# A selective-scan kernel: softplus from exp(v) taken out of PSUM, and the old y added where y is copied out

## The chip, the cores and the metric

The kernel runs on one core of one Trainium2 chip. The metric is device microseconds (us) of one execution: 11103.35 us before the change, the median of 3 runs (11099.11 to 11105.88). A core has TensorE (PE, matrix multiply; PEld is its loading of weights), VectorE (DVE), ScalarE (ACT, table functions), GpSimd (POOL), and SyncE (SP), whose queue issues the DMAs. Each engine works through its own instructions in order and waits for others by semaphores. SBUF is the on-chip memory of 128 partitions; PSUM is the memory that TensorE writes.

## The reference

Two layers of a vision state-space model, four images each, all in float32. The first layer takes nearly all of the time and is the one changed. For each image (64 x 64 positions, L = 4096) it normalizes, projects 192 channels to 384, and runs a selective scan in four directions k: by rows, by columns, and both backwards. The scan is

```python
delta = jax.nn.softplus(delta + delta_bias[None, :, None])
...
def step(h, inp):
    dt, ut, bt, ct = inp
    dA = jnp.exp(dt[..., None] * A_k[None])
    dBu = dt[..., None] * bt[:, :, None, :] * ut[..., None]
    h = dA * h + dBu
    y = jnp.einsum('bkdn,bkn->bkd', h, ct)
    return (h, y)
```

with 16 states n for each of 384 channels d. The y of the four directions are summed with u times D, normalized, multiplied by silu(z) and projected back. The second layer does the like with a convolution ahead and has a form of the scan of its own.

## The kernel before

`FirstLayer.run` alternates, image by image, between a stage `between` (finish the last image, project the next one) and a stage `scans`. `scans` is the subject here: it takes four stretches of some 2200 us each.

The work of one image in `scans` is 32 items. An item is one direction k and one chunk c of 512 positions; the 384 channels are ND = 3 groups of 128 partitions. Items come in pairs (k, i) and (k + 2, 7 - i), first for k = 0 and 2 (rows), then for k = 1 and 3 (columns); so item 16 of each image is the first that goes by columns. An item is 16 steps, one for each state n. The whole is written as one loop over g = 16 * item + n, and the order of instructions on PE, ACT, DVE and POOL is that in which the loop writes them (`manual_schedule`). The order on SP is left to the planner of the framework.

One step g does this:

- ACT: `b_product(g + 2)` (L716, four instructions) multiplies delta*u by B into `xT`; `decay(g + 1)` (L728, three) makes exp(delta * A) into `a`.
- PE: `turn_x(g + 1, d)` (L733) transposes `xT` into a PSUM tile `x` for each of the three channel groups; each is written after `scan(g, d)`, whose buffer it takes.
- DVE: `scan(g, d)` (L741), three instructions, h = a*h + x along the 512 positions, and a small reduction (L751) that keeps the last column as the carry for the next chunk.
- POOL: `c_product(g)` (L755) multiplies h by C in place. SP loads the rows of C for two steps at a time into `bct` (L721), each load waiting for POOL to free one of three buffers.
- PE: `add_y` (L768) transposes h of a step at least LAG = 3 steps back into the three PSUM tiles `yp`, accumulating over the 16 states: 12 transposes a step. None is done in step 3 of an item, and two steps' worth in step 4, because the `yp` of the last item are still being copied out.

Beside that, two things happen once per item.

**Old y.** y lies in DRAM and each item adds to its rows. `start_y` (L762) opens the accumulation in steps 3 and 4 by multiplying the tile `yold`, loaded from DRAM, with the identity into `yp`. `end_y` (L781) copies `yp` to `yt` on DVE in steps 2 and 3 of the next item, and SP stores it. `yold` has one buffer. It is loaded one item ahead (in the loop's order after step 5), except where the direction turns from rows to columns: there the rows to be read are spread over what the last items stored, so the load is issued in step 3, after the last `end_y`.

**Delta.** `Item.steps` lists what prepares an item's delta, by (items ahead, step, engine). v is `dp`, a matmul of 13 rows (L632) into a PSUM tile of the pool `ps_m`, two buffers shared with other small uses. softplus(v) is computed as max(v, 0) + log(1 + e) with e = exp(-|v|), the log with a correction for the rounding of 1 + e. Two items ahead: ACT takes |v| in steps 10 to 12 (L638) and the exponential in step 13 (L641), POOL makes wl = 1 + e in step 14 (L645) and dt = wl - 1 in step 15 (L649). One item ahead: ACT takes the log of wl in step 2 (L652), POOL e - dt in step 1 (L655) and adds wl in step 4 (L658); DVE `delta` (L661) computes max(v, 0) + e in steps 7 to 9, from v made a second time on PE in steps 5 to 7. The tile `e` has one buffer: the |v| of an item waits for the last `delta` of the item before it. Then delta is transposed and multiplied by u (L675, L681) in steps 10 to 13.

In the first 8 items of an image, PE and ACT also compute z for the gate (`gate_in`, `gate_out`, L794, three ACT instructions an item).

Of the kernel before, what the change touches and what calls it, by code (L numbers as in the profile page):

```python
# [10 lines left out]
F32 = mybir.dt.float32  # L11
AF = mybir.ActivationFunctionType
ALU = mybir.AluOpType
# [4 lines left out]
ND = DI // 128  # L18
CB, NC2 = 96, 2
LC = 512  # L20
# [382 lines left out]
class FirstLayer:  # L403
# [168 lines left out]
    def scans(self):  # L572
        nc, tc = self.tc.nc, self.tc
        with ExitStack() as ctx:
            pool = lambda name, bufs, **k: ctx.enter_context(tc.tile_pool(name=name, bufs=bufs, **k))
            p1, p2, p3, p7 = pool("b1", 1), pool("b2", 2), pool("b3", 3), pool("b7", 7)
            pk = pool("ca", 2)
            ps_y = pool("psy", 1, space=bass.MemoryType.PSUM)
            ps_x = pool("psx", 3, space=bass.MemoryType.PSUM)
            ps_m = pool("psm", 2, space=bass.MemoryType.PSUM)  # L580
            ident = self.ident
            n8 = LC // HW

            def along(ap, k):
# [5 lines left out]
            def rows(tile_, dram, k, c):  # L590

                if k % 2 == 0:
                    return [(tile_, dram[c * LC : (c + 1) * LC, :].rearrange("(j p) e -> p j e", p=128))]
                v = dram.rearrange("(h w) e -> w h e", w=HW)[c * n8 : (c + 1) * n8]
                v = v.rearrange("(j s) h e -> s h j e", s=2)
                return [(tile_[s * HW : (s + 1) * HW], v[s]) for s in range(2)]

            def load(name, dram, k, c):
                t = p1.tile([128, NJ, DI], F32, name=name)
                for to, of in rows(t, dram, k, c):  # L600
                    nc.sync.dma_start(to, of)
                return t

            class Item:
# [27 lines left out]
                    nc.tensor.matmul(self.dp[d], w, self.xd[0 : DR + 1, :], start=True, stop=True)  # L632


                def absolute(self, d):
                    if d == 0:
                        self.e = p1.tile([128, ND, LC], F32, name="e")
                    nc.scalar.activation(self.e[:, d, :], self.dp[d], AF.Abs)  # L638

                def exp(self):  # L640
                    nc.scalar.activation(self.e, self.e, AF.Exp, scale=-1.0)  # L641

                def plus(self):
                    self.wl = p1.tile([128, ND, LC], F32, name="wl")
                    nc.gpsimd.tensor_scalar(self.wl, self.e, 1.0, 1.0, ALU.add, ALU.mult)  # L645

                def minus(self):
                    self.dt = p2.tile([128, ND, LC], F32, name="dt")
                    nc.gpsimd.tensor_scalar(self.dt, self.wl, -1.0, 1.0, ALU.add, ALU.mult)  # L649

                def log(self):
                    nc.scalar.activation(self.wl, self.wl, AF.Ln)  # L652

                def rest(self):
                    nc.gpsimd.tensor_tensor(self.e, self.e, self.dt, ALU.subtract)  # L655

                def total(self):
                    nc.gpsimd.tensor_tensor(self.e, self.e, self.wl, ALU.add)  # L658

                def delta(self, d):  # L660
                    nc.vector.scalar_tensor_tensor(  # L661
                        self.dt[:, d, :], self.dp[d], 0.0, self.e[:, d, :], ALU.max, ALU.add
                    )

                def load_u(self):
# [19 lines left out]
                def steps(self):  # L685

                    s = lambda f, *a: (lambda: f(*a))
                    r = [(3, 12, "pool", self.load_rows), (2, 0, "pe", self.turn_b), (2, 1, "dve", self.keep_b)]
                    for d in range(ND):
                        r += [(2, 7 + d, "pe", s(self.dt_rows, d)), (2, 10 + d, "act", s(self.absolute, d))]  # L690
                    r += [(2, 13, "act", self.exp), (2, 14, "pool", self.plus), (2, 14, "pool", self.load_u)]
                    r += [(2, 15, "pool", self.minus), (1, 2, "act", self.log)]
                    r += [(1, 1, "pool", self.rest), (1, 4, "pool", self.total)]
                    for d in range(ND):
                        r += [(1, 5 + d, "pe", s(self.dt_rows, d)), (1, 7 + d, "dve", s(self.delta, d))]
                    for b in range(ND):
                        r += [(1, 10 + b, "pe", s(self.turn, b)), (1, 11 + b, "dve", s(self.times_u, b))]
                    return r
# [4 lines left out]
            items = []  # L703
# [50 lines left out]
                it, n = flat[g]  # L754
                nc.gpsimd.tensor_tensor(hs[g], hs[g], bc(cs[g - n % 2][:, n % 2, :], 1, ND), ALU.mult)  # L755

            def start_y(it, b):

                if b == 0:
                    it.yp = [ps_y.tile([128, LC], F32, name=f"yp{i}") for i in range(ND)]  # L760
                yo = it.yold.rearrange("p j e -> p (j e)")[:, b * LC : (b + 1) * LC]
                nc.tensor.matmul(it.yp[b], ident, yo, start=True, stop=False, skip_group_check=True)  # L762

            def add_y(g, b):
                it, n = flat[g]
                for i in range(NJ):
                    j, d = divmod(b * NJ + i, ND)
                    nc.tensor.matmul(  # L768
                        it.yp[b][:, i * 128 : (i + 1) * 128],
                        hs[g][:, d, j * 128 : (j + 1) * 128],  # L770
                        ident,
                        start=False,
                        stop=n == NS - 1,
                        is_transpose=True,
                        skip_group_check=True,
                    )

            def end_y(it, b):
                if b == 0:
                    it.yt = p1.tile([128, NJ, DI], F32, name="yt")  # L780
                nc.vector.tensor_copy(it.yt.rearrange("p j e -> p (j e)")[:, b * LC : (b + 1) * LC], it.yp[b])  # L781
                if b == ND - 1:
                    for of, to in rows(it.yt, self.y_dram, it.k, it.c):
                        nc.sync.dma_start(to, of)
# [13 lines left out]
            with tc.manual_schedule(engines={nc.tensor.engine, nc.scalar.engine, nc.vector.engine, nc.gpsimd.engine}):  # L798
# [15 lines left out]
                        if e == engine:  # L814
                            f()

                items[0].yold = load("yold", self.y_dram, items[0].k, items[0].c)
                c_rows(0)
                b_product(0)
                b_product(1)  # L820
# [3 lines left out]
                LAG = 3  # L824
                late = []
                for g in range(N + LAG + 1):
                    i, n = divmod(g, NS)
                    it = items[i] if g < N else None
                    before = items[i - 1] if i > 0 else None
                    prepare(g, "act")  # L830
                    if g + 2 < N:
                        if g % 2 == 0:
                            c_rows(g + 2)
                        b_product(g + 2)
                    if g + 1 < N:
                        decay(g + 1)
                    adds = [[] for _ in range(ND)]
                    if it is not None:
                        for at, b in (((LAG, 1), 0), ((LAG, 2), 1), ((LAG + 1, 0), 2)):
                            if at[0] == n:  # L840
                                adds[at[1]].append((start_y, it, b))

                    ready = [x for x in late if x <= g - LAG and (n > LAG or x // NS < i)][:2]
                    for j, (x, b) in enumerate((x, b) for x in ready for b in range(ND)):
                        adds[j // len(ready)].append((add_y, x, b))
                    late = [x for x in late if x not in ready]
                    for d in range(ND):
                        if g < N:
                            scan(g, d)
                        if d == 1:  # L850
                            prepare(g, "dve")
                        if before is not None and (n, d) in ((LAG - 1, 2), (LAG, 0), (LAG, 1)):
                            end_y(before, {2: 0, 0: 1, 1: 2}[d])
                            if (n, d) == (LAG, 1) and it is not None and it.yold is None:
                                it.yold = load("yold", self.y_dram, it.k, it.c)
                        if g + 1 < N:
                            turn_x(g + 1, d)
                        for f, *a in adds[d]:
                            f(*a)
                    if g < N:  # L860
                        prepare(g, "pe")
                        c_product(g)
                        late.append(g)
                        prepare(g, "pool")
                        if n == 5 and i + 1 < len(items) and items[i + 1].k % 2 == it.k % 2:
                            q = items[i + 1]
                            q.yold = load("yold", self.y_dram, q.k, q.c)


    def finish(self, batches):  # L870
# [762 lines left out]
```

## Time and profile before

| what | value |
|---|---|
| median of 3 runs | 11103.35 us |
| profiled execution, its own time | 11106.54 us |
| its span, first to last instruction | 11104.6 us |
| mean granted TensorE clock | 0.939 |
| busy: DVE, ACT, PE, POOL | 9693.3, 9775.8, 9551.9, 8587.9 us |
| items | 128, of 16 steps each |
| scans on DVE (L741) | 6144 of about 1.2 us |

The profile is one execution taken by the hardware profiler. A group of instructions is given as line, engine, operation, out<-in with the program's tile names, shapes and count; then busy us and mean ns of one; then the idle time of the engine just before them and what ended it. Instructions of one engine overlap a little, so that the mean of one is larger than the busy time over the count. In the list of waits a line reads "who waited <- for whom: us in total, times, longest". One fp32 matmul is two PE instructions in the records. The engines' shares are averages over stages; the stages between the images are other work.

### The profile page before, as it was taken

What the parts mean: (1) busy time and instruction counts of PE and PEld (TensorE: products, weight loads), DVE (VectorE), ACT (ScalarE), POOL (GpSimd) and SP (SyncE); (2) the same over time, 40 slices, a digit from 0 to 9 for tenths busy, and PEclk for the clock granted to TensorE, in tenths of its full rate; (3) what the DMA queues carried; (4) which work ended last, traced back from release to release, by engine and by line L of the source; (5) the groups of instructions that cost most, each with busy time, mean ns of one, the idle gap of its engine ahead of it and who ended that gap; (6) DMA issues with size and microseconds to landing.
All of it is one profiled execution on the core that took longest, in us unless ns stands there. A gap on an engine that the chain in (4) does not pass through costs nothing. (4 is left out here: it accounts for less than half of the span.)

```text
span 11104.6 us, 172135 instructions
## 1 busy us (share of the span) xinstructions
PE 9551.9 (86%) x61449; PEld 7273.6 (66%) x61449; DVE 9693.3 (87%) x11515; ACT 9775.8 (88%) x16979; POOL 8587.9 (77%) x2776
## 2 busy tenths in 40 slices
PE   7998888888988888888988888889988888788677
PEld 4776666666776666656776666657766766655366
DVE  4999899976999899968999899949998999878675
ACT  5999999977999999969999999959999999856477
POOL 3999899955999899938999899929998999700370
PEclk8999999998999999998999999989999999989688
DMA  4333344344333344443333433353333434433458
GB/s 125 109 108 101 91 101 101 98 137 127 109 106 101 92 101 99 98 159 112 109 103 96 98 97 99 93 168 109 109 99 95 98 98 98 120 119 123 157 131 272
DMA packets 833671, 1267.54 MB, mean 114 GB/s; under 512 B 102026, under 2 KB 517655, under 8 KB 832292
## 3 DMA queue, kind: packets, MB, share of 16 engines
q1 hardware_dynamic: 827940, 1250.15, 40.5%
q0 software_dynamic: 4864, 6.29, 0.4%
q8 instruction: 488, 8.00, 0.3%
q14 instruction: 379, 3.10, 0.1%
HBM read 955.83 MB, written 300.42 MB: 113 GB/s over the span
## 5 line engine op out<-in xcount | busy, mean ns | idle before, releaser
L755 POOL TENSOR_TENSOR h<-h,bct 128x1536 f32<-128x1536 f32 x2048 | 7062.9, 3470 | 579.9 <-DVE carry L751 477.5
L741 DVE TENSOR_TENSOR_SCAN h<-a,carry,x 128x512 f32<-128x512 f32 x5376 | 6604.9, 1266 | 231.0 <-PE x L733 194.9
L733 PE MATMUL x<-ident,xT 128*128 128x128 f32 x24576 | 4000.8, 287 | 811.8 <-DVE h L741 710.1
L716 ACT ACTIVATE xT<-dtuT,bT 128x384 f32<-128x384 f32 x8192 | 4358.8, 609 | 93.0 <-PE x L733 87.3
L733 PEld LDWEIGHTS x<-ident,xT 128*128 128x128 f32 x24576 | 2804.0, 145 | 2136.5 <-DVE h L741 920.5
L728 ACT ACTIVATE a<-dt,A_log_f 128x512 f32<-128x512 f32 x6144 | 3977.7, 716 | 0.0
L768 PE MATMUL yp<-ident,h 128*128 128x128 f32 x24576 | 3703.1, 277 | 9.2 <-POOL h L755 9.2
L768 PEld LDWEIGHTS yp<-ident,h 128*128 128x128 f32 x24576 | 2944.2, 144 | 78.8 <-issue 62.6
L632 PE MATMUL dp<-xd,w_dtb_f 13*128 13x512 f32 x1536 | 882.7, 657 | 216.0 <-DVE dt L661 211.3
L741 DVE TENSOR_TENSOR_SCAN h<-a,x 128x512 f32<-128x512 f32 x768 | 899.1, 1207 | 191.3 <-PE x L733 114.0
L645 POOL TENSOR_SCALAR wl<-e 128x1536 f32<-128x1536 f32 x128 | 189.2, 1478 | 799.3 <-ACT e L641 406.2
L519 PE MATMUL pp<-xT,w_in 96*128 96x512 f32 x1152 | 539.2, 617 | 1.1 <-DVE xw L562 1.1
L632 PEld LDWEIGHTS dp<-xd,w_dtb_f 13*128 13x128 f32 x1536 | 235.0, 189 | 456.6 <-DVE dt L661 341.3
L762 PE MATMUL yp<-yold,ident 128*128 128x512 f32 x768 | 445.1, 664 | 72.7 <-DMA yold<-y 72.7
L1137 DVE SCALAR_TENSOR_TENSOR acc<-pad,conv_w_s,acc 128x2048 f32<-128x2048 f32 x192 | 439.3, 2342 | 53.5 <-ACT acc L1135 52.9
L638 ACT ACTIVATE e<-dp 128x512 f32<-128x512 f32 x384 | 224.7, 585 | 269.3 <-DVE dt L661 155.4
L1118 POOL MEMSET pad<- 128x66 f32 x12 | 1.9, 158 | 578.4 <-DVE acc L1137 458.9
L658 POOL TENSOR_TENSOR e<-e,wl 128x1536 f32<-128x1536 f32 x128 | 445.1, 3477 | 0.3
L655 POOL TENSOR_TENSOR e<-e,dt 128x1536 f32<-128x1536 f32 x128 | 442.9, 3460 | 0.3
L751 DVE TENSOR_REDUCE carry<-h 128x3 f32<-128x3 f32 x2048 | 322.7, 158 | 70.4
L519 PEld LDWEIGHTS pp<-xT,w_in 96*128 96x128 f32 x1152 | 221.3, 198 | 244.4 <-issue 234.3
L661 DVE SCALAR_TENSOR_TENSOR dt<-dp,e 128x512 f32<-128x512 f32 x384 | 255.5, 666 | 65.2 <-POOL e L658 58.7
(170 smaller groups left out, 6875.3 us busy)
## 6 DMA issues: line engine op xcount, KB each, us to landing
bct<-xp SPq DMA_DIRECT2D x1024, 512.0 KB, 4.9
uT<-uT SPq DMA_DIRECT2D x64, 768.0 KB, 4.7
yold<-y SPq DMA_DIRECT2D x64, 768.0 KB, 7.9
y<-yt SPq DMA_DIRECT2D x64, 768.0 KB, 4.5
uT<-uT SPq DMA_DIRECT2D x128, 384.0 KB, 5.0
yold<-y SPq DMA_DIRECT2D x128, 384.0 KB, 5.3
y<-yt SPq DMA_DIRECT2D x128, 384.0 KB, 4.6
zg<-gate SPq DMA_DIRECT2D x64, 768.0 KB, 6.3
```

Of the source, the lines that this page charges most:

```text
L519: self.tc.nc.tensor.matmul(pp, self.w_in[:, i, e * 128 : (e + 1) * 128], self.xT[:, i, t * LC : (t + 1) * LC], start=(i == 0), stop=(i == ...
L632: nc.tensor.matmul(self.dp[d], w, self.xd[0 : DR + 1, :], start=True, stop=True)
L655: nc.gpsimd.tensor_tensor(self.e, self.e, self.dt, ALU.subtract)
L658: nc.gpsimd.tensor_tensor(self.e, self.e, self.wl, ALU.add)
L716: nc.scalar.mul(xTs[g][:, j, :], it.dtuT[:, j * DI : (j + 1) * DI], it.bT[:, j, n : n + 1])
L728: nc.scalar.activation(as_[g][:, d, :], it.dt[:, d, :], AF.Exp, scale=scale)
L733: nc.tensor.transpose(xs[g, d][:, j * 128 : (j + 1) * 128], xTs[g][:, j, d * 128 : (d + 1) * 128], ident)
L741: nc.vector.tensor_tensor_scan(along(hs[g][:, d, :], it.k), along(as_[g][:, d, :], it.k), along(xs.pop((g, d)), it.k), 0.0 if it.first els ...
L755: nc.gpsimd.tensor_tensor(hs[g], hs[g], bc(cs[g - n % 2][:, n % 2, :], 1, ND), ALU.mult)
L762: nc.tensor.matmul(it.yp[b], ident, yo, start=True, stop=False, skip_group_check=True)
L768: nc.tensor.matmul(it.yp[b][:, i * 128 : (i + 1) * 128], hs[g][:, d, j * 128 : (j + 1) * 128], ident, start=False, stop=n == NS - 1, is_tr ...
L1137: nc.vector.scalar_tensor_tensor(acc, part(tap), weight(tap), acc, ALU.mult, ALU.add)
```

## The change

In softplus, e becomes exp(v) instead of exp(-|v|), taken by ACT straight out of PSUM in steps 10 to 12, where |v| was taken. The exponential over 1536 columns in step 13 is gone. POOL takes m = min(e, 1) in step 13 and dt = (m + 1) - 1 in step 15; ACT takes log(e + 1), with the one as a bias, in step 2; POOL's two tensor operations give the correction m - dt and its sum with the log. `delta` becomes max(min(that, 30), v). The steps of the other operations stay.

The matmuls of `start_y` are gone: the first `add_y` of an item starts the accumulation, and `end_y` on DVE adds `yold` where it copied before. `yold` is loaded in step 8 of the item that it belongs to, for every item alike, and is read in steps 2 and 3 of the next one.

```diff
-                def absolute(self, d):
+                def exp(self, d):
                     if d == 0:
                         self.e = p1.tile([128, ND, LC], F32, name="e")
-                    nc.scalar.activation(self.e[:, d, :], self.dp[d], AF.Abs)
-
-                def exp(self):
-                    nc.scalar.activation(self.e, self.e, AF.Exp, scale=-1.0)
-
-                def plus(self):
-                    self.wl = p1.tile([128, ND, LC], F32, name="wl")
-                    nc.gpsimd.tensor_scalar(self.wl, self.e, 1.0, 1.0, ALU.add, ALU.mult)
-
-                def minus(self):
+                    nc.scalar.activation(self.e[:, d, :], self.dp[d], AF.Exp)
+
+                def cap(self):
+                    self.m = p1.tile([128, ND, LC], F32, name="m")
+                    nc.gpsimd.tensor_scalar(self.m, self.e, 1.0, 1.0, ALU.min, ALU.mult)
+
+                def rounded(self):
                     self.dt = p2.tile([128, ND, LC], F32, name="dt")
-                    nc.gpsimd.tensor_scalar(self.dt, self.wl, -1.0, 1.0, ALU.add, ALU.mult)
+                    nc.gpsimd.tensor_scalar(self.dt, self.m, 1.0, -1.0, ALU.add, ALU.add)
 
                 def log(self):
-                    nc.scalar.activation(self.wl, self.wl, AF.Ln)
+                    nc.scalar.activation(self.e, self.e, AF.Ln, bias=one)
 
                 def rest(self):
-                    nc.gpsimd.tensor_tensor(self.e, self.e, self.dt, ALU.subtract)
+                    nc.gpsimd.tensor_tensor(self.m, self.m, self.dt, ALU.subtract)
 
                 def total(self):
-                    nc.gpsimd.tensor_tensor(self.e, self.e, self.wl, ALU.add)
+                    nc.gpsimd.tensor_tensor(self.e, self.e, self.m, ALU.add)
 
                 def delta(self, d):
                     nc.vector.scalar_tensor_tensor(
-                        self.dt[:, d, :], self.dp[d], 0.0, self.e[:, d, :], ALU.max, ALU.add
+                        self.dt[:, d, :], self.e[:, d, :], 30.0, self.dp[d], ALU.min, ALU.max
                     )
...
-                        r += [(2, 7 + d, "pe", s(self.dt_rows, d)), (2, 10 + d, "act", s(self.absolute, d))]
-                    r += [(2, 13, "act", self.exp), (2, 14, "pool", self.plus), (2, 14, "pool", self.load_u)]
-                    r += [(2, 15, "pool", self.minus), (1, 2, "act", self.log)]
+                        r += [(2, 7 + d, "pe", s(self.dt_rows, d)), (2, 10 + d, "act", s(self.exp, d))]
+                    r += [(2, 13, "pool", self.cap), (2, 14, "pool", self.load_u)]
+                    r += [(2, 15, "pool", self.rounded), (1, 2, "act", self.log)]
...
-            def start_y(it, b):
-
-                if b == 0:
-                    it.yp = [ps_y.tile([128, LC], F32, name=f"yp{i}") for i in range(ND)]
-                yo = it.yold.rearrange("p j e -> p (j e)")[:, b * LC : (b + 1) * LC]
-                nc.tensor.matmul(it.yp[b], ident, yo, start=True, stop=False, skip_group_check=True)
-
             def add_y(g, b):
                 it, n = flat[g]
+                if n == 0 and b == 0:
+                    it.yp = [ps_y.tile([128, LC], F32, name=f"yp{i}") for i in range(ND)]
                 for i in range(NJ):
...
-                        start=False,
+                        start=n == 0 and i == 0,
...
-                nc.vector.tensor_copy(it.yt.rearrange("p j e -> p (j e)")[:, b * LC : (b + 1) * LC], it.yp[b])
+                part = slice(b * LC, (b + 1) * LC)
+                yt, yo = (t.rearrange("p j e -> p (j e)")[:, part] for t in (it.yt, it.yold))
+                nc.vector.tensor_add(yt, it.yp[b], yo)
...
-                items[0].yold = load("yold", self.y_dram, items[0].k, items[0].c)
...
-                        for at, b in (((LAG, 1), 0), ((LAG, 2), 1), ((LAG + 1, 0), 2)):
-                            if at[0] == n:
-                                adds[at[1]].append((start_y, it, b))
...
-                            if (n, d) == (LAG, 1) and it is not None and it.yold is None:
-                                it.yold = load("yold", self.y_dram, it.k, it.c)
...
-                        if n == 5 and i + 1 < len(items) and items[i + 1].k % 2 == it.k % 2:
-                            q = items[i + 1]
-                            q.yold = load("yold", self.y_dram, q.k, q.c)
+                        if n == 8:
+                            it.yold = load("yold", self.y_dram, it.k, it.c)
```

More of the change, by code (lines that the diff above doesn't have):

```diff
@@ L580, in scans @@
             ps_m = pool("psm", 2, space=bass.MemoryType.PSUM)
-            ident = self.ident
+            ident, one = self.ident, self.one
             n8 = LC // HW
@@ L837, in scans @@
                     adds = [[] for _ in range(ND)]
-                    if it is not None:
-                        for at, b in (((LAG, 1), 0), ((LAG, 2), 1), ((LAG + 1, 0), 2)):
-                            if at[0] == n:
-                                adds[at[1]].append((start_y, it, b))
                     ready = [x for x in late if x <= g - LAG and (n > LAG or x // NS < i)][:2]
```

## The prediction

> **What bounds the kernel.** I read the page's shares first:
>
> ```profile
> PE 9551.9 (86%) x61449; PEld 7273.6 (66%) x61449; DVE 9693.3 (87%) x11515; ACT 9775.8 (88%) x16979; POOL 8587.9 (77%) x2776
> ```
>
> Four engines lie close together, so shares alone choose no bound. The windows view, with one window from the first scan of an item to that of the next, goes further: item 2 (which has a gate), item 12, item 21, and item 16, the first by columns.
>
> ```profile
> 319.80:390.90 71.10, 64.22 (x433) 50.87 (x432) 66.17 (x75) 69.00 (x122) 64.62 (x21) 0.95 0.40 106
> 1011.60:1080.30 68.70, 60.06 (x419) 47.29 (x419) 65.61 (x75) 66.31 (x118) 64.73 (x21) 0.98 0.37 99
> 1643.20:1710.30 67.10, 58.43 (x419) 45.64 (x420) 65.46 (x76) 65.16 (x116) 64.74 (x21) 1.00 0.41 101
> 1283.70:1369.90 86.20, 62.77 (x419) 48.98 (x420) 63.10 (x75) 65.53 (x117) 64.54 (x20) 0.84 0.33 87
> ```
>
> Columns: window, length, busy us of PE, PEld, DVE, ACT, POOL, granted clock, DMA. Item 21, at full clock, lasts 67.10 us with DVE busy 65.46: little is left. Item 12 has 3.1 us of DVE idle. Item 2 has ACT at 69.00 of 71.10. Item 16 loses some 18 us outright. The waits view says for what:
>
> ```profile
> DVE h L741 <- PE x L733: 308.9, 446, 18.0
> ACT e L638 <- DVE dt L661: 155.4, 108, 2.6
> PE yp L762 <- DMA yold<-y: 72.7, 4, 18.4
> ```
>
> DVE waits for transposes, not for ACT; ACT itself waits once an item, at the first |v| of step 10, for the single buffer `e`. So an ordinary item is DVE's, and ACT is a close second. The timeline of item 16 shows the third line:
>
> ```profile
> 1307.42 17.54 SPq L601 DMA_DIRECT2D yold<-y  x4
> ...
> 1317.03 2.07 PE L762 MATMUL yp<-yold,ident 128*128 128x512 f32 x2 [18.07 <-DMA yold<-y]
> ...
> 1320.06 1.22 DVE L741 TENSOR_TENSOR_SCAN h<-a,x 128x512 f32<-128x512 f32 x1 [17.70 <-PE x L733]
> ```
>
> The load is issued after the last `end_y`, behind a `bct` load in SP's queue; `start_y` waits for it at the head of PE's queue, the transposes behind it, and DVE for those.
>
> The prices, from the groups of instructions:
>
> ```profile
> L762 PE MATMUL yp<-yold,ident 128*128 128x512 f32 x768 | 445.1, 664 | 72.7 <-DMA yold<-y 72.7
> L681 DVE TENSOR_TENSOR dtuT<-tp,uT 128x512 f32<-128x512 f32 x384 | 259.0, 674 | 18.8 <-PE tp L675 8.7
> L781 DVE COPY yt<-yp 128x512 f32<-128x512 f32 x384 | 258.2, 674 | 17.7 <-PE yp L768 17.4 <-issue 0.3
> L645 POOL TENSOR_SCALAR wl<-e 128x1536 f32<-128x1536 f32 x128 | 189.2, 1478 | 799.3 <-ACT e L641 406.2 <-DMA xp<-xw 393.1
> L641 ACT ACTIVATE e<-e 128x1536 f32<-128x1536 f32 x128 | 189.2, 1478 | 0.3
> ```
>
> Last, two windows of 3.4 us in step 3 of item 11:
>
> ```profile
> 954.40:957.80 3.40, 1.26 (x11) 0.85 (x9) 3.40 (x4) 3.40 (x7) 3.40 (x2) 1.00 0.22 71
> 957.80:961.20 3.40, 3.40 (x10) 1.98 (x9) 3.37 (x5) 3.40 (x7) 3.40 (x2) 0.50 0.98 281
> ```
>
> PE was busy for 1.26 us (37%); the next window ran at half clock.
>
> **What the Trainium skill says.** "TensorE: Matmul & The Clock Gate", section "What's actually happening": the clock is halved after a quiet window of a free-running 3413 ns grid and restored after a busy one. The trace agrees: changes come in steps of 3.413 us. From its clock and matmul records I worked out the thresholds here, leaving L632's 13-row matmuls aside: all 62 full-clock windows of the scans with PE busy below 35% were followed by half clock, 68 of 82 at 35 to 40%, 6 of 44 at 40 to 45%, nearly none above 50%. At half clock, all 75 windows busy below 80% were followed by another at half. "VectorE: DVE Perf Modes", "Why PSUM operands drop a tier": with a PSUM operand, fp32 runs at one element a cycle; hence a copy from PSUM should cost what an addition costs, and L781 and L681 are both 674 ns. "ScalarE: Activation LUTs", "What ACT_TABLE_LOAD costs": functions cost alike, a pointer operand about 93 ns more; L638 without one is 585 ns, L794 with a bias pointer 681.
>
> **The change, part by part**, against the profiled 11106.5 us (span 11104.6 and 1.9 around it; 3.2 above the median).
>
> 1. *The stall at the turn to columns goes.* The load no longer gates PE: it has from step 8 to step 2 of the next item, over 40 us, and its median landing takes 5 to 8 us. Item 16 averages 85.2 us over the four images. Without the wait I put it at 66.7, between item 30 (65.9, almost nothing prepared) and the usual 68.2. Gain 4 x 18.5 = 74. Bounds: 17.7 and 20 an item, 70 to 80.
>
> 2. *ACT loses L641 and gains a pointer*: -1.48 + 0.09 = -1.39 us an item. In items 8 to 29, which are DVE's (DVE idle 2.6 us an item, of it about 1.65 for PE in steps 9 to 11), this lengthens ACT's wait at `e` and gives almost nothing; 0.1 for the small gaps in steps 1 and 5, x 84 = 8. Items 1 to 7 are ACT's: they average 69.3 us with 3.9 us of DVE idle, the excess of 1.3 lying in steps 0, 1, 3 and 5. I take 1.1 x 28 = 31 (bounds 0.6 and 1.3: 17 to 36). Exp from PSUM costs what |v| did.
>
> 3. *Start of each image*: `e` lies on the path to the first scan twice (item 0's delta; item 1's exponential ahead of `b_product(0)` on ACT), 1.48 each: 4 x 2.96 = 12.
>
> 4. *DVE*: three additions for three copies, and `delta` with its operands exchanged (the second layer's L1376 also reads SBUF first and PSUM second: 678 ns against L661's 666). Nothing; 0.01 us x 6 x 128 = 8 at most. There is no cover for this on DVE.
>
> 5. *POOL*: two one-input operations for two, 1.48 each; the first a step earlier. POOL runs without a pause from step 14 to about step 9, and `total` (L658) ends a median 0.4 us ahead of `delta`. Starting at step 13 rather than 14 uses one step's slack, 3.77 - 3.47 = 0.30, so the margin becomes 0.7 us. The log no longer waits for POOL's second operation (20.4 us in all, hidden). Minimum on POOL is nowhere in this trace: below, 1.48; above, the two-input 3.47. I take 1.48.
>
> 6. *PE loses* six L762 records an item, 445.1/128 = 3.5 us, in steps 3 and 4. PE is behind only in steps 4 to 6 there (DVE's wait in step 5: 0.05 us, counted above); the waits of steps 9 to 11 start from L632, which waits for the `delta` that frees `ps_m`. They stay. But step 3 becomes emptier. In item 12 PE is free from 1024.06 to the transposes of step 4 at 1029.9, but for three groups of transposes of 0.63 us, 1.8 apart; a window there holds two, 1.26 us. By the thresholds nearly nine items in ten will go to half clock in or just after step 3, where 34 of 127 did. Half clock from about 1028.3 or later ends after one window, and PE, 3 us less loaded than before, still meets its scans. If it starts earlier (1.3 of the 3.41 us of phase, 38%), its first window stays under 80% busy, and half clock lasts 6.8 us, through step 4. There 4 transposes take 0.86: from 1029.87 come 4 transposes and 8 adds to 1032.5, 4 to 1033.3, 8 to about 1034.7, and the third group of x is there at 1035.3, against the scan's 1034.85. Some 0.5 us late: 0.38 x 0.5 x 128 = 25 lost. Bounds: 0, and 0.9 in every item, 115.
>
> 7. *SP*: as many loads as before; in the built programs `yold` stands at the same place in SP's queue for row items (after the store of `yt` and one `bct`). Nothing queued behind it moves.
>
> Sum: -74 - 8 - 31 - 12 + 25 = -100: 11006 for a profiled execution, 11003 as a median; I say 11000, 0.9% faster.
>
> **Rivals.** (a) *ACT is the bound throughout.* Then every item gains 1.39: 124 x 1.39 = 172, with 74 and 12: 10850. For it: ACT has the largest share. Against: item 21, DVE 65.46 of 67.10, and ACT waiting in step 10. (b) *Half clock spreads*: the 0.9 us of part 6 in every item takes back 115: -125 + 115, about 11090. For it: some six in ten items more come into that state, and DVE has no slack. Against: PE's work in step 4 falls by 2 us. (c) *PE's relief shortens the waits of steps 9 to 11* too, or half clock costs nothing: 0.4 x 124 more, 10950. (d) *Slower: the minimum on POOL.* At 3.47 us, `total` passes its 0.7 us margin by 1.3 and `delta`, DVE's own instruction, waits as much in every item: 124 x 1.3 = 161, so 11106 - 100 + 161 - 3 = 11164. It costs from 2.2 us on and cancels the gain at 3.0. "GPSIMD Engine Reference", "Elementwise — side-by-side cycle accounting", has bodies of up to two operations at about one cycle per element, which fits L645's 1478 ns, but data-dependent branches at 12; I hold a minimum for the former. (e) That `yold` is still waited for: it would show as before, 70 us worse; the 40 us speak against it.
>
> **Chances.** My forecast 0.66, with its own range 10965 to 11045; (a) 0.05; (b) 0.11; (c) 0.10; (d) 0.07; (e) 0.01. The range to hold 8 in 10: 10935 to 11080. About 0.2%, 22 us, is what a measurement of this kernel can tell from no change. Faster: the forecast, (a), (c), and half of (b), 0.87; within: the rest of (b), 0.06; slower: 0.07.
>
> **What will show it.** Right: no wait of PE for `yold`, item 16 under 68 us, items 1 to 7 at about 68, L781's mean near 674 and POOL's new L645 near 1478, a lower mean clock than 0.939 with half clock in step 3 of most items, and ACT's wait at `e` grown to about 3 us. Wrong: `delta` waiting for POOL (d), DVE waiting for x in step 5 by nearly 1 us (b), or ordinary items at 67 or less (a, c).

## The result, and the profile after

The changed kernel takes 11943.1 us, the median of 4 runs (11940.04 to 11948.4), against 11101.23 us for the kernel before in the same comparison. The ratio is 1.0762, 95% interval 1.0749 to 1.0775: 7.6% slower, where 0.9% faster was forecast.

The first line of the page after, the shares of the engines over the span of 11938.1 us:

```profile
PE 9833.7 (82%) x60681; PEld 7595.2 (64%) x60681; DVE 9746.0 (82%) x11515; ACT 9643.7 (81%) x16851; POOL 9572.8 (80%) x2776
```

DVE and ACT are busy for about as long as before. POOL has as many instructions, 2776, and 985 us more. The groups say which (line, engine, operation, out<-in, shapes, count, then busy us and mean ns, then idle time before and its releaser):

```profile
L647 POOL TENSOR_SCALAR dt<-m 128x1536 f32<-128x1536 f32 x128 | 690.8, 5397 | 0.7
L643 POOL TENSOR_SCALAR m<-e 128x1536 f32<-128x1536 f32 x128 | 689.5, 5387 | 780.1 <-ACT e L639 398.3 <-DMA xp<-xw 381.8
...
L776 DVE TENSOR_TENSOR yt<-yp,yold 128x512 f32<-128x512 f32 x384 | 258.8, 675 | 21.4 <-PE yp L761 17.9 <-issue 0.7
L659 DVE SCALAR_TENSOR_TENSOR dt<-e,dp 128x512 f32<-128x512 f32 x384 | 257.3, 671 | 406.8 <-POOL e L656 400.2 <-PE dp L632 6.5
```

The two one-input operations on POOL, `cap` (L643) and `rounded` (L647), take 5.39 and 5.40 us each, where L645 and L649 took 1.48. The addition of the old y (L776) costs what the copy cost, 675 ns, and `delta` 671. The windows view of one ordinary item, 20, from its first scan to that of the next (window, length, busy us of PE, PEld, DVE, ACT, POOL, clock, DMA):

```profile
1698.40:1774.50 76.10, 62.54 (x413) 49.84 (x414) 66.16 (x76) 65.01 (x117) 72.44 (x21) 0.91 0.34 89
```

Items 18 to 29 last 76.00 us on average against 68.18 before. DVE's work in one has hardly changed, 66.16 us (65.46 and 65.61 in the two items shown before); POOL is now the longest, at 72.44, but not without a pause: it too stands for 3.7 us of the item. The waits view shows how POOL's work reaches DVE, first in the changed kernel (who waited <- for whom: us in total, times, longest):

```profile
DVE h L739 <- PE x L731: 739.8, 744, 4.9
...
DVE dt L659 <- POOL e L656: 400.2, 123, 23.3
...
PE yp L761 <- POOL h L753: 311.7, 128, 4.3
```

and in the kernel before:

```profile
DVE dt L661 <- POOL e L658: 58.7, 4, 16.9
...
PE yp L768 <- POOL h L755: 9.2, 8, 2.2
```

Both waits come once an item now. The two timelines of item 20, POOL's and then the one of the engines that follow it, give the order:

```profile
1682.38 3.47 POOL L753 TENSOR_TENSOR h<-h,bct 128x1536 f32<-128x1536 f32 x1 [1.09 <-DVE carry L749]
1686.81 3.47 POOL L753 TENSOR_TENSOR h<-h,bct 128x1536 f32<-128x1536 f32 x1 [0.95 <-DVE carry L749]
1691.11 3.47 POOL L753 TENSOR_TENSOR h<-h,bct 128x1536 f32<-128x1536 f32 x1 [0.83 <-DVE carry L749]
1694.56 5.38 POOL L643 TENSOR_SCALAR m<-e 128x1536 f32<-128x1536 f32 x1
1699.92 6.89 POOL L753 TENSOR_TENSOR h<-h,bct 128x1536 f32<-128x1536 f32 x2
1706.78 5.39 POOL L647 TENSOR_SCALAR dt<-m 128x1536 f32<-128x1536 f32 x1
```

```profile
1722.37 10.26 POOL L753 TENSOR_TENSOR h<-h,bct 128x1536 f32<-128x1536 f32 x3
...
1725.87 0.66 PE L761 MATMUL yp<-ident,h 128*128 128x128 f32 x4 [2.91 <-POOL h L753]
...
1727.07 1.28 DVE L739 TENSOR_TENSOR_SCAN h<-a,carry,x 128x512 f32<-128x512 f32 x1 [2.60 <-PE x L731]
...
1732.58 3.45 POOL L656 TENSOR_TENSOR e<-e,m 128x1536 f32<-128x1536 f32 x1
...
1736.07 0.69 DVE L659 SCALAR_TENSOR_TENSOR dt<-e,dp 128x512 f32<-128x512 f32 x1 [1.94 <-POOL e L656]
```

Just before step 13 POOL has caught up and waits for DVE; from step 13 on it falls behind. By step 6 its products are late, so `add_y` waits at the head of PE's queue, the transposes of x behind it, and a scan behind those; in step 7 `delta` waits for `total`. So what counts is not how busy POOL is over the item, but how late it is where others wait for it. The stall at the turn to columns is gone all the same: item 16 lasts 73.7 us, less than its neighbours.

### The profile page after: what moved, and what is told of

Its sections match the earlier page's. It is cut to its first block, busy times and chain, and to the rows that moved or that the text cites. A ratio compares the mean times of both kernels' runs of the same rounds, so it can differ in the third digit from the quotient of the medians.

```text
span 11938.1 us, 170647 instructions
## 1 busy us (share of the span) xinstructions
PE 9833.7 (82%) x60681; PEld 7595.2 (64%) x60681; DVE 9746.0 (82%) x11515; ACT 9643.7 (81%) x16851; POOL 9572.8 (80%) x2776
## 5 line engine op out<-in xcount | busy, mean ns | idle before, releaser
L731 PE MATMUL x<-ident,xT 128*128 128x128 f32 x24576 | 4230.5, 299 | 1206.7 <-DVE h L739 1111.3
L731 PEld LDWEIGHTS x<-ident,xT 128*128 128x128 f32 x24576 | 2973.3, 151 | 2492.8 <-DVE h L739 1220.8
L761 PE MATMUL yp<-ident,h 128*128 128x128 f32 x24576 | 3963.0, 291 | 311.7 <-POOL h L753 311.7
L761 PEld LDWEIGHTS yp<-ident,h 128*128 128x128 f32 x24576 | 3173.2, 152 | 342.3 <-POOL h L753 342.0
L643 POOL TENSOR_SCALAR m<-e 128x1536 f32<-128x1536 f32 x128 | 689.5, 5387 | 780.1 <-ACT e L639 398.3
L632 PE MATMUL dp<-xd,w_dtb_f 13*128 13x512 f32 x1536 | 1022.9, 755 | 153.4 <-DVE dt L659 148.8
L647 POOL TENSOR_SCALAR dt<-m 128x1536 f32<-128x1536 f32 x128 | 690.8, 5397 | 0.7
L659 DVE SCALAR_TENSOR_TENSOR dt<-e,dp 128x512 f32<-128x512 f32 x384 | 257.3, 671 | 406.8 <-POOL e L656 400.2
L653 POOL TENSOR_TENSOR m<-m,dt 128x1536 f32<-128x1536 f32 x128 | 444.2, 3470 | 0.3
L656 POOL TENSOR_TENSOR e<-e,m 128x1536 f32<-128x1536 f32 x128 | 442.7, 3459 | 0.3
```

What stands on the lines that cost most here:

```text
L643: nc.gpsimd.tensor_scalar(self.m, self.e, 1.0, 1.0, ALU.min, ALU.mult)
L647: nc.gpsimd.tensor_scalar(self.dt, self.m, 1.0, -1.0, ALU.add, ALU.add)
L653: nc.gpsimd.tensor_tensor(self.m, self.m, self.dt, ALU.subtract)
L656: nc.gpsimd.tensor_tensor(self.e, self.e, self.m, ALU.add)
L731: nc.tensor.transpose(xs[g, d][:, j * 128 : (j + 1) * 128], xTs[g][:, j, d * 128 : (d + 1) * 128], ident)
L761: nc.tensor.matmul(it.yp[b][:, i * 128 : (i + 1) * 128], hs[g][:, d, j * 128 : (j + 1) * 128], ident, start=n == 0 and i == 0, stop=n == N ...
```

## The experiments

**1. The price of a pair of operations.** A row of POOL instructions on a scratch tile was put at the end of the kernel before:

```diff
+    with tc.tile_pool(name="probe", bufs=1) as pp:
+        src = pp.tile([128, 1536], F32, name="src")
+        nc.gpsimd.memset(src, 0.5)
+        nc.gpsimd.tensor_scalar(pp.tile([128, 1536], F32, name="q_add_mult"), src, 1.0, 1.0, ALU.add, ALU.mult)
...
+        nc.gpsimd.tensor_scalar(pp.tile([128, 1536], F32, name="q_min"), src, 1.0, None, ALU.min)
...
+        nc.gpsimd.tensor_scalar(pp.tile([128, 512], F32, name="q512_min_mult"), src[:, :512], 1.0, 1.0, ALU.min, ALU.mult)
```

> The kernel before with a row of POOL instructions on a scratch tile put at its end, one for each pair of operations, to price the forms by themselves. If the pair of operations sets the price: (add, mult) about 1.48 us on 1536 columns; (min, mult) and (add, add) about 5.4 us, as in the changed kernel; the 512-column ones a third of that and a fixed part. If POOL's price in the changed kernel comes from its surroundings (what else uses SBUF at the time) and not from the form, all pairs cost about 1.48 us here. Which single operations are cheap is open. Total: before, and some 60 us for the row.

The one execution took 11166.31 us, 61 more than the kernel before. Its groups, one instruction each; the tile's name tells the pair:

```profile
L1547 POOL TENSOR_SCALAR q_min_mult<-src 128x1536 f32<-128x1536 f32 x1 | 5.4, 5393 | 0.0
L1549 POOL TENSOR_SCALAR q_add_add<-src 128x1536 f32<-128x1536 f32 x1 | 5.4, 5392 | 0.0
...
L1555 POOL TENSOR_SCALAR q_add<-src 128x1536 f32<-128x1536 f32 x1 | 4.1, 4077 | 0.0
...
L1564 POOL TENSOR_SCALAR q_add_add<-src 128x512 f32<-128x512 f32 x1 | 1.9, 1921 | 0.0
...
L1545 POOL TENSOR_SCALAR q_add_mult<-src 128x1536 f32<-128x1536 f32 x1 | 1.5, 1464 | 0.0
L1550 POOL TENSOR_SCALAR q_mult_mult<-src 128x1536 f32<-128x1536 f32 x1 | 1.5, 1463 | 0.0
L1546 POOL TENSOR_SCALAR q_mult_add<-src 128x1536 f32<-128x1536 f32 x1 | 1.5, 1462 | 0.0
...
L1565 POOL TENSOR_SCALAR q_add_mult<-src 128x512 f32<-128x512 f32 x1 | 0.6, 607 | 0.0
```

| operations on 1536 columns | us |
|---|---|
| (add, mult), (mult, add), (mult, mult) | 1.46 |
| (add, add), (min, mult), (max, mult), (mult, min), (add, min), (subtract, mult), (mult, subtract), (add, subtract) | 5.37 to 5.39 |
| one operation alone: min, add or mult | 4.08 |
| two tensors: add or subtract | 3.41 |

The price hangs on the pair: in these 72 us PE, DVE and ACT together were busy for under 5. A column costs (1464 - 607)/1024 = 0.84 ns in a cheap pair and (5392 - 1921)/1024 = 3.39 ns in a dear one. A single operation is dearer than a pair with a multiplication by 1.

**2. The two halves apart.** One kernel takes only the half with the old y, the other only softplus; each is the diff of the change, cut in two.

```diff
-            def start_y(it, b):
...
-                nc.vector.tensor_copy(it.yt.rearrange("p j e -> p (j e)")[:, b * LC : (b + 1) * LC], it.yp[b])
+                nc.vector.tensor_add(yt, it.yp[b], yo)
```

> Only the half of the change that concerns the old y; softplus as before. Theory 1 (POOL's two one-input operations are the whole loss): the forecast of this half stands, 74 us gained at the turn to columns, up to 25 lost to half clock: about 11030 to 11050. Theory 2 (the emptier step 3 and its half clock, or the late load of the old y, are a good part of the loss): slower than before, 11200 or more.

```diff
-                    nc.gpsimd.tensor_scalar(self.wl, self.e, 1.0, 1.0, ALU.add, ALU.mult)
...
+                    nc.gpsimd.tensor_scalar(self.m, self.e, 1.0, 1.0, ALU.min, ALU.mult)
...
+                    nc.gpsimd.tensor_scalar(self.dt, self.m, 1.0, -1.0, ALU.add, ALU.add)
```

> Only the softplus half; the old y as before. Theory 1: all of the loss is here: about 840 above before and some 50 to 70 more for the stall that is back, 11990 to 12010, unless the stall hides in POOL's backlog. Theory 2: under 11700.

The y half: 11078.56 us against 11104.97, ratio 0.9972 (0.9961 to 0.9984), a gain of 26 us and not 55 to 75. The softplus half: 11954.24, ratio 1.0765 (1.0747 to 1.0783). So the loss lies in the second. The y half has the stall's gain (item 16 from 85.17 to 65.77 us), but its items 8 to 15 are 0.76 us longer than before and items 18 to 29 0.48, and half clock begins in step 3 or 4 of 126 of its 128 items: more is lost there than the 25 us forecast. The softplus half is also faster than was expected of it (11990 to 12010): it keeps the stall of item 16 (91.8 us), yet its other items are some 0.2 to 1.0 us shorter than those of the changed kernel. Less half clock goes with that (mean clock 0.915 against 0.891); that it is the reason was not tried.

**3. Only the form of the two operations.** First, the changed kernel with both in the form (add 0, mult 1):

```diff
-                    nc.gpsimd.tensor_scalar(self.m, self.e, 1.0, 1.0, ALU.min, ALU.mult)
+                    nc.gpsimd.tensor_scalar(self.m, self.e, 0.0, 1.0, ALU.add, ALU.mult)
...
-                    nc.gpsimd.tensor_scalar(self.dt, self.m, 1.0, -1.0, ALU.add, ALU.add)
+                    nc.gpsimd.tensor_scalar(self.dt, self.m, 0.0, 1.0, ALU.add, ALU.mult)
```

> The changed kernel with both one-input POOL operations in the form (add 0, mult 1), so that m = e and dt = e and the correction of the log's rounding is left out; same number, order and shapes of instructions. Theory 1: POOL's two at 1.48 us again and the forecast comes true: 10960 to 11045. Theory 3 (the new order of softplus, the exponential out of PSUM or the earlier first POOL operation is the cause, not the price of the form): stays near 11900.

11048.16 us, ratio 0.9948 (0.9931 to 0.9965): 3 us above the window that theory 1 gave, and 895 us below the changed kernel. Then one of the two dear:

```diff
-                    nc.gpsimd.tensor_scalar(self.dt, self.m, 1.0, -1.0, ALU.add, ALU.add)
+                    nc.gpsimd.tensor_scalar(self.dt, self.m, 0.0, 1.0, ALU.add, ALU.mult)
```

> The changed kernel with the first POOL operation left as it is, (min, mult), and the second as (add 0, mult 1), so that the correction comes to nothing: one of the two at 5.39 us. If POOL's chain has a margin of 0.7 us an item and each microsecond beyond it is one of the item's: 3.91 - 0.7 = 3.2 in 124 items over 11048, about 11445. If the slack that POOL has in steps 10 to 14 takes up more of it: under 11250. If each slow operation cost half of the whole: 11495.

11421.25 us, ratio 1.0287 (1.0271 to 1.0303): 373 us over the run with none, 3.0 an item where 3.2 were expected; the second dear operation adds 522 more, 4.2 an item. The first costs less than the 3.91 us by which it is dearer, as a chain with a margin has it. The second costs more than that. With one, `delta` waits for `total` in every item (347.5 us in all, 124 times), but PE waits only 10.4 us for POOL's h; its 311.7 us come with the second. What else is in the 0.3 us was not tried. Last, the reverse, the kernel before with its pairs changed and nothing else:

```diff
-                    nc.gpsimd.tensor_scalar(self.wl, self.e, 1.0, 1.0, ALU.add, ALU.mult)
+                    nc.gpsimd.tensor_scalar(self.wl, self.e, 1.0, 0.0, ALU.add, ALU.add)
...
-                    nc.gpsimd.tensor_scalar(self.dt, self.wl, -1.0, 1.0, ALU.add, ALU.mult)
+                    nc.gpsimd.tensor_scalar(self.dt, self.wl, -1.0, 0.0, ALU.add, ALU.add)
```

> The kernel before with one thing changed: its two POOL operations add 0 where they multiplied by 1, so (add, add) for (add, mult), with the same values. If the pair's price is the cause by itself: POOL has 7.82 us more an item, its margin before delta is 0.4, so 7.4 in 124 items, 920 more, about 12020, less up to 70 where the stall of item 16 hides in it. If the loss of the changed kernel needed something else of the change: well under 11900.

11946.06 us, ratio 1.0768 (1.075 to 1.0785), as slow as the changed kernel, by one constant and one opcode in each of two instructions, with the same values. That is 847 us more than before, where 920, less up to 70, were expected; the stall did not hide (item 16 lasts 92.65 us), and items 18 to 29 are 7.16 us longer, not 7.4. Its groups:

```profile
L649 POOL TENSOR_SCALAR dt<-wl 128x1536 f32<-128x1536 f32 x128 | 689.2, 5384 | 0.7
L645 POOL TENSOR_SCALAR wl<-e 128x1536 f32<-128x1536 f32 x128 | 689.1, 5383 | 795.1 <-ACT e L641 600.5 <-DMA xp<-xw 194.6
...
L652 ACT ACTIVATE wl<-wl 128x1536 f32<-128x1536 f32 x128 | 189.8, 1483 | 829.9 <-POOL dt L649 829.9
```

Here the wait sits elsewhere: ACT's log writes the tile that POOL's second operation reads, and ACT stands for 829.9 us. Where the wait shows depends on the order of softplus; that there is one comes from POOL's price, since nothing else was changed.

**4. The change with cheap pairs.** m = (e + 1) * 1, dt = (m - 1) * 1, the log of m in place, the correction e - dt; the cap at 1 is left out.

```diff
-                    nc.gpsimd.tensor_scalar(self.m, self.e, 1.0, 1.0, ALU.min, ALU.mult)
+                    nc.gpsimd.tensor_scalar(self.m, self.e, 1.0, 1.0, ALU.add, ALU.mult)
...
-                    nc.gpsimd.tensor_scalar(self.dt, self.m, 1.0, -1.0, ALU.add, ALU.add)
+                    nc.gpsimd.tensor_scalar(self.dt, self.m, -1.0, 1.0, ALU.add, ALU.mult)
...
-                    nc.scalar.activation(self.e, self.e, AF.Ln, bias=one)
+                    nc.scalar.activation(self.m, self.m, AF.Ln)
...
-                    nc.gpsimd.tensor_tensor(self.m, self.m, self.dt, ALU.subtract)
+                    nc.gpsimd.tensor_tensor(self.e, self.e, self.dt, ALU.subtract)
```

> The changed kernel with POOL's two operations written in the pairs that the probe found cheap: m = (e + 1) * 1, dt = (m - 1) * 1, the log of m in place, e - dt as the correction. The cap at 1 is left out: for v above 0 the correction is then that of 1 + e itself, at most half a unit in the last place of e. Theory 1 (the price of the form is the whole loss): as with both in (add, mult) before, 11048, within 15. If the missing correction of that run, or its log beside POOL, had helped it: nearer to 11100.

11038.68 us, ratio 0.9949 (0.9936 to 0.9963). This is the change without its cap, 65 us faster than the kernel before. To the same kernel three matmuls were added in step 3, one after each group of transposes, into a tile that is overwritten:

```diff
+            def warm(it):
+                if it.yp is None:
+                    it.yp = [ps_y.tile([128, LC], F32, name="yp0")]
+                nc.tensor.matmul(it.yp[0], ident, it.dt[:, 0, :], start=True, stop=True)
...
+                    if n == LAG and it is not None:
+                        for d in range(ND):
+                            adds[d].append((warm, it))
```

> The last kernel, and three matmuls of 512 columns in step 3 of each item, one after each group of transposes, into a PSUM tile that the next accumulation overwrites: PE does as much as in the kernel before, but nothing waits for it. If half clock after the emptied step 3 costs the 0.5 to 0.8 us that ordinary items are longer than before: 60 to 90 less than the last, 10960 to 10990, and no half clock in steps 3 and 4. If half clock there costs only what DVE is seen to wait in step 5 (0.17 to 0.3 us): 20 to 35 less, 11015 to 11030. If it costs nothing: no less, or a little more for the added matmuls.

11009.08 us, ratio 0.9919 (0.9906 to 0.9933), 30 us less for more work. In the run of part 3 with both pairs cheap, half clock began in step 3 or 4 of 124 of 128 items (37 in the kernel before), and so it did in the kernel with cheap pairs; here in none. The windows view of item 20, first without, then with the added matmuls:

```profile
1556.40:1626.00 69.60, 60.20 (x413) 48.85 (x414) 65.93 (x76) 65.36 (x118) 64.62 (x21) 0.93 0.40 97
```

```profile
1546.40:1615.20 68.80, 60.54 (x419) 47.16 (x420) 65.67 (x76) 65.07 (x117) 64.61 (x21) 0.98 0.41 98
```

DVE's work is the same within 0.3 us; the clock is 0.98 for 0.93 and the item 0.8 shorter. On average items 8 to 15 and 18 to 29 are 0.40 us shorter and items 1 to 7 0.65; DVE's idle time in step 5, 0.26 to 0.45 us an item, falls to 0.03. In total the 30 us fit the second of the run's expectations, but they are a difference: these items gain some 50 us, while items 16 and 17 become 1.3 and 1.7 us longer and the stretches between and after the images some 12 in all. So half clock seems to cost an ordinary item rather more than DVE's wait in step 5.

**5. Two versions that leave out more.** With the added matmuls kept, the second v on PE and DVE's three deltas were dropped, first together with POOL's four operations, then without those:

```diff
+                def log(self):
+                    self.dt = p2.tile([128, ND, LC], F32, name="dt")
+                    nc.scalar.activation(self.dt, self.e, AF.Ln, bias=one)
...
-                    for d in range(ND):
-                        r += [(1, 5 + d, "pe", s(self.dt_rows, d)), (1, 7 + d, "dve", s(self.delta, d))]
```

> The last kernel with delta = log(exp(v) + 1) written by ACT straight into dt: POOL's four operations, DVE's three deltas, the second v on PE and with them the correction of the log's rounding and the guard for large v are left out. If DVE bounds an ordinary item, with the waits of steps 9 to 11 that start from the delta: 3 x 0.57 of DVE and 1.65 of waits fewer in 124 items, 420 less, about 10550. If ACT takes over at its 65.3 us an item: about 330 less, 10650. If POOL's load were the bound even at 1.48 us: over 10 us an item less.

```diff
-                    nc.gpsimd.tensor_tensor(self.e, self.e, self.m, ALU.add)
+                    nc.gpsimd.tensor_tensor(self.dt, self.e, self.m, ALU.add)
...
-                    for d in range(ND):
-                        r += [(1, 5 + d, "pe", s(self.dt_rows, d)), (1, 7 + d, "dve", s(self.delta, d))]
```

> The kernel with the cheap pairs and the three added matmuls, in which POOL's last operation writes log + correction straight into dt: DVE's three deltas and the second v on PE go, the correction of the log's rounding stays, the guard for large v is left out. If the gain of the log-only kernel came from DVE and from the waits of steps 9 to 11, and not from POOL's four operations: 10580 to 10650, the rest being POOL's chain. If POOL's 10 us an item were what was gained there: near 11009 less the 210 of DVE, 10800.

10576.56 us, ratio 0.9526 (0.9512 to 0.9541), and 10601.92 us, ratio 0.9554 (0.9538 to 0.9569). The first lies between what was expected with DVE as the bound (10550) and with ACT (10650); the second lies where it should if POOL's operations were not what was gained. The windows view of item 20 of the first and of the second:

```profile
1475.30:1540.30 65.00, 56.83 (x413) 44.54 (x414) 63.59 (x72) 65.00 (x118) 55.47 (x16) 1.00 0.47 104
```

```profile
1486.00:1550.90 64.90, 56.83 (x413) 44.55 (x414) 63.58 (x73) 64.90 (x118) 64.52 (x21) 1.00 0.44 104
```

ACT is busy without a pause in both, so it is the bound there, at 65 us; POOL's four operations, 9 us of an item, cost an ordinary item nothing at their cheap prices. The 25 us between the two come from the start of the images (38 us longer in the second; the rest is 13 shorter). The second keeps the correction of the log's rounding, but lacks the cap at 1 and the guard for large v. That matters: worked out in fp32, the correction is off by up to 2 for about half of the v from 16.6 to 17.3, which the maximum with v hides in the kernel with cheap pairs and nothing hides here. As timings, both beat the kernel before and the changed one.

## Why the prediction was wrong

**The step that failed is part 5, "two one-input operations for two, 1.48 each".** It took shape, type and number of inputs as the form of the instruction, and the pair of operations as free. The pair decides: 5.39 us for both. The upper bound of that part, the two-input price of 3.47, was no bound, and it was put on the minimum alone; (add, add) was not questioned, though only (add, mult) had been seen. The section of the Trainium skill that rival (d) quotes ("GPSIMD Engine Reference", "Elementwise — side-by-side cycle accounting") has up to two operations at about one cycle per element; the probe shows that price for three of eleven pairs: 1.46 us, and 0.84 ns a column for (add, mult), which was tried at two lengths. "Performance pitfalls for Q7 kernels" on the same page lists 4 cycles per element for a chain of dependent fp32 operations; with the 1.2 GHz of its "Specifications" I estimate 3.3 ns from that, close to the 3.39 measured. That the dear pairs run in such a chain is not shown.

**Rival (d) had the mechanism.** It named the place (`total`, then `delta`), the margin (0.7 us) and the rule (each microsecond beyond it is lost in each item). With the measured price: 2 x (5.39 - 1.48) - 0.7 = 7.1 us in 124 items, 883 over the 11048 of the run with cheap pairs, 11931; measured 11943. It missed the wait one step earlier, of PE's `add_y` for POOL's h, which belongs to the same chain. That its sum comes so close with that wait left out is in part luck: the first dear operation cost 0.2 us an item less than the rule says, the second 0.3 more. It was given 0.07, and only for the minimum.

**The other terms,** seen in the kernel with cheap pairs (span 11031.4 against 11104.6), from the mean lengths of its items:

| term | forecast us | measured us | how |
|---|---|---|---|
| stall at the turn to columns | -74 | -78 | item 16: 85.17 to 65.58, x 4 |
| item 17 | 0 | -11 | 68.31 to 65.62, x 4 |
| items 1 to 7, ACT's relief | -31 | 0; -18 with the clock kept up | 69.33 to 69.33; to 68.68; x 28 |
| ordinary items, half clock and small gaps | +17 | +40; +5 with the clock kept up | 8 to 15 +0.41, 18 to 29 +0.53, 30 +0.41 |
| start of each image | -12 | -17 | first scan 1.7 earlier, three times 5.1 between images |

The measured column sums to -66 of the 73 us by which the span is shorter. With the clock kept up, the first two rows are -73 and -4.

Part 1 (the stall) was right, parts 3 (the start) and 4 nearly so: L776 for L781 takes 675 ns for 674. Part 6 was right in kind and too small: half clock in step 3 or 4 of 97% of the items ("nearly nine in ten"), and ordinary items 40 us longer in all where 17 were forecast. Its thresholds come out of the trace in kind: between the first and last scan of each image I count 50 of 50 full-clock windows below 35% followed by half clock, 73 of 79 at 35 to 40% and 5 of 43 at 40 to 45%. Part 2 took the DVE idle time of items 1 to 7 for ACT's. In step 3 it was: 0.38 us an item there falls to 0.06. In step 1 it was not: 0.6 us stands there before and after, though ACT has 1.5 us less to do, and in the timeline PE's gate matmuls come between the transposes. What step 3 gained is taken back by longer waits for the transposes in steps 5 and 11 (0.14 and 0.21 us), so the sum stays at 3.9. So the relief is there, 0.38 us against the y half alone, in which these items are as much longer than before. That half clock takes it back is suggested by the run with the added matmuls, where they gain 0.65. Item 17 waited 0.84 us in step 3 and 1.61 in step 5 before, 0.03 and 0.23 in the kernel with cheap pairs; most of the second goes with the y half alone. Why it waited is not shown.

## What to carry to other kernels

An instruction's price belongs to the operation too, not only to its shape and its inputs: when an edit changes an opcode on POOL and no row of the trace has that very pair, price it by itself in a run before counting on it. A multiplication by 1 that looks idle may be what makes a form cheap. And where an engine has under a microsecond of margin at the place where others wait for it, count what is added against that margin, not against the engine's idle time: POOL's 64.6 us and 7.8 more would have fitted into 72.4 us, but the item took 76.

## What the runs showed of the hardware

- POOL, one input, 1536 fp32 columns: 1.46 us for pairs made of add and mult with at least one mult, 5.37 to 5.39 for the eight others that were tried, 4.08 for a single operation; 3.41 for adding or subtracting two tensors (the probe, one instruction each; in the kernels 5.38 to 5.40 for dear pairs and 1.48 to 1.49 for cheap ones, over 128 instructions each).
- TensorE's clock: three matmuls an item whose result nobody reads, 3.1 us of work, made the kernel 30 us faster. Half clock began in step 3 or 4 of 124 of 128 items without them and of none with them.
